# Layer 0's queries made for two blocks of 256 tokens at once

## The chip, the cores and the metric

The kernel runs on one core of one Trainium2 chip. A core has five engines that run their own instruction streams [...]: TensorE (PE in the profile, its weight loads PEld), VectorE (DVE), ScalarE (ACT), GpSimd (POOL) and SyncE (SP), which here only issues transfers. The metric is the device time of one execution in microseconds (us); lower is better.

## The reference

Two transformer layers over x of 2 sequences x 2048 tokens x 512 features, in float32. The change is in layer 0's cross-attention to a context of 128 tokens per sequence:

```
q = layer_norm(_layernorm(x), ln_g, ln_b) @ Wq      # 16 heads of 64
k, v = (layer_norm(ctx) @ Wk, layer_norm(ctx) @ Wv)
q, k = rope(q), rope(k)
aw = 30 * tanh((q . k / 8) / 30), masked (causal, padding)
x = x + (softmax(aw) @ v) @ Wo
```

Then follow a quantised feed-forward layer (its step for x is taken from the largest absolute value of all normalised tokens, so it can't start before the last token of the attention is done), and layer 1 with a second cross-attention and a feed-forward layer of eight experts.

## The kernel before

Everything is in `two_layers`. x lies in 32 SBUF tiles of 128 tokens, `xs[n]`. Layer 0's attention walks over blocks of 256 tokens (`B0`, two tiles each): 16 blocks, the two sequences in turns. A block has 4 units, one for each group `g` of 4 heads, so there are 64 units, and a loop over `u` from 0 to 65 writes down by hand the order in which PE, DVE, ACT and POOL get their instructions (`manual_schedule`); only the transfers on SP are placed by the framework. Each engine works through its list in order.

What one pass of the loop issues:

- `scores(u)` (L413): 16 small products into the first half of the PSUM tile `sc`; ACT then takes tanh (L418) and exp (L420) of them. For the first block of each sequence POOL applies the causal mask (L422).
- `queries(u + 2, par)` (L392): the queries of the unit two ahead, even and odd dimensions (`par` 0 and 1) apart. Each is 4 products of 128 features x 256 tokens (each is two instructions in the trace, since the data are float32). DVE multiplies with the rope tables (L397, L398, L401, L403), POOL combines them to `q0`, `q1` (L402, L404).
- `mixed(u - 1)` (L434): row sums and weighted values into the second half of `sc`; DVE takes the reciprocal (L440) and multiplies (L441) to `att`. `sc` is one tile, so the next scores wait for L441, and the mix waits for the tanh of the unit before it in the order.
- `projected(u - 2, t)` (L450): the unit's part of the output projection, for the block's two tiles `t`. The four units of a block are summed in one PSUM tile `pw` for each of the two tiles of tokens.
- after the last unit of a block, `finished` adds `pw` to x (L458) and takes mean and variance (L91); `largest` normalises and takes the largest absolute value (L467).

The queries need the normalised x by feature (features on partitions). For the first two blocks `first_blocks` normalises by token (`center`, L103) and PE transposes (L369), ACT adds gain and bias on the way out of PSUM (L378). For the other 14 blocks a copy of x by feature is loaded (`features_in`, 512 KB); `normed` takes the statistics, writes them through DRAM (`turned_in`, L343), and they come back spread over all partitions (`along`); POOL subtracts the mean (`centered`, L349), DVE multiplies (`scaled`, L349), ACT applies gain and bias. In between, DVE quantises the rows of the feed-forward weights (`makes`: `gate_up`, `down`; L278 to L284), 26 in all, and SP turns them by transfer into `wgT`, `wuT` and `wdT`. `steps_along` (L472, L476) spreads the down weights' steps.

After the loop, layer 1's keys (L660) fill PE while `act_step` takes the maximum over all tokens (L622 to L633), from which the feed-forward layer's first products (L743) are made ready.

Two lines that matter for the order:

```
                if u + 2 < nu:
                    queries(u + 2, 0)
                elif 1 < u < nu:
                    projected(u - 2, 0)
```

Of the kernel before, what the change touches and what calls it, by code (L numbers as in the profile page):

```python
# [54 lines left out]
NB0 = B0 // P  # L55
BF = 512
# [6 lines left out]
def two_layers(ctx: ExitStack, tc: tile.TileContext, a, out):  # L63
# [86 lines left out]
    with ExitStack() as l0:  # L150
# [16 lines left out]
        order = [b * TPB + j * NB0 + t for j in range(TPB // NB0) for b in range(B) for t in range(NB0)]  # L167
# [24 lines left out]
        for n in order[:NB0]:  # L192
            load(xs[n], x_in[n])
        xnTs = {}

        def features_in(k):

            xnTs[k] = mid.tile([P, ND, B0], F32, name="xnT", bufs=3)
            load(xnTs[k], a["x_turned"][k // B, k % B])
# [13 lines left out]
        def tables_in(j):  # L213
            tabs[j] = []
            for name in ("rope_cos", "rope_sin"):
                tab = mid.tile([P, B0], F32, name=name)
                load(tab, a[name][:, j * B0 : (j + 1) * B0])
                tabs[j].append(tab)
# [100 lines left out]
        blocks = [(j, b) for j in range(S // B0) for b in range(B)]  # L319
        tiles = [[b * TPB + j * NB0 + t for t in range(NB0)] for j, b in blocks]  # L320
        nu = len(blocks) * NG
        stats, along, ropes, qs, prs, atts, pws = {}, {}, {}, {}, {}, {}, {}
        stat_dram = dram.tile([len(blocks), NB0, 2, P], F32, name="stat_dram")
# [3 lines left out]
        def normed(k):  # L327


            stats[k] = small.tile([P, NB0, 2], F32, name="stat")  # L330
            for t, n in enumerate(tiles[k]):
                mv = variance(xs[n])
                ve = small.tile([P, 1], F32, name="ve")
                nc.vector.tensor_scalar(ve, mv[:, 1:2], 1.0 + EPS, EPS * EPS, ALU.mult, ALU.add)
                nc.vector.tensor_copy(stats[k][:, t, 0:1], mv[:, 0:1])
                nc.gpsimd.tensor_tensor(stats[k][:, t, 1:2], ve, minus_half, ALU.pow)
            if k > 1:
                features_in(k)
                turned_in(k)

        def turned_in(k):

            nc.sync.dma_start(out=stat_dram[k].rearrange("t s p -> p (t s)"), in_=stats[k].rearrange("p t s -> p (t s)"))  # L343
            along[k] = mid.tile([P, NB0, 2, P], F32, name="along", bufs=1)
            load(along[k], stat_dram[k].partition_broadcast(P))

        def by_token(k, i, op, engine):
            x = xnTs[k].rearrange("p c (t q) -> p c t q", t=NB0)
            engine.tensor_tensor(x, x, along[k][:, :, i].unsqueeze(1).to_broadcast([P, ND, NB0, P]), op)  # L349

        def centered(k):
            by_token(k, 0, ALU.subtract, nc.gpsimd)

        def scaled(k):
            by_token(k, 1, ALU.mult, nc.vector)

        def first_blocks(k):

            xn = mid.tile([P, NB0, D], F32, name="xn", tag="xnT", bufs=3)
            for t, n in enumerate(tiles[k]):  # L360
                center(xn[:, t, :], xs[n], stats[k][:, t, 0:1], stats[k][:, t, 1:2])
            xnTs[k] = mid.tile([P, ND, B0], F32, name="xnT", bufs=3)

            def rest():
                for c0 in range(0, ND, 2):
# [6 lines left out]
                    affine(k, c0, pt)  # L372
# [3 lines left out]
        def affine(k, c0, pt=None):  # L376
            for c in range(c0, c0 + 2):
                nc.scalar.activation(  # L378
                    xnTs[k][:, c, :], xnTs[k][:, c, :] if pt is None else pt[:, c - c0, :], AF.Identity, bias=lnb[:, c : c + 1], scale=lng[:, c : c + 1]
                )  # L380

        def queries(u, par):

            k, g = divmod(u, NG)
            j, b = blocks[k]
            if par == 0:
                if j not in tabs:
                    tables_in(j)
                ropes[u] = [mid.tile([P, B0], F32, name=f"rt{i}", bufs=1) for i in range(4)]
            pq, rt = psm.tile([P, B0], F32, name="pq", tag="m"), ropes[u]  # L390
            for c in range(ND):
                nc.tensor.matmul(  # L392
                    pq, wqs[c // 2][:, c % 2, par, g * P : (g + 1) * P], xnTs[k][:, c, :], start=(c == 0), stop=(c == ND - 1)
                )
            cos, sin = tabs[j]
            if par == 0:
                nc.vector.tensor_tensor(rt[0], pq, cos, ALU.mult)  # L397
                nc.vector.tensor_tensor(rt[1], pq, sin, ALU.mult)  # L398
                return
            qs[u] = [mid.tile([P, B0], F32, name=f"q{i}") for i in range(2)]  # L400
            nc.vector.tensor_tensor(rt[2], pq, sin, ALU.mult)  # L401
            nc.gpsimd.tensor_tensor(qs[u][0], rt[0], rt[2], ALU.subtract)  # L402
            nc.vector.tensor_tensor(rt[3], pq, cos, ALU.mult)  # L403
            nc.gpsimd.tensor_tensor(qs[u][1], rt[3], rt[1], ALU.add)  # L404

        def scores(u):

            k, g = divmod(u, NG)
            j, b = blocks[k]
            for par, k_ in ((0, kTe), (1, kTo)):  # L410
                for h in range(4):
                    rows = slice(32 * h, 32 * h + 32)
                    nc.tensor.matmul(  # L413
                        sc[:, h, :B0], k_[rows, g, b * T : (b + 1) * T], qs[u][par][rows, :],
# [6 lines left out]
            if j == 0:  # L421
# [5 lines left out]
        def mixed(u):  # L427

            k, g = divmod(u, NG)
            b = blocks[k][1]  # L430
            atts[u] = mid.tile([P, 2, B0], F32, name="att")
# [7 lines left out]
            rd = mid.tile([P, B0], F32, name="rd", bufs=1)  # L439
            nc.vector.reciprocal(rd, sc[:, 0, B0:])  # L440
            nc.vector.tensor_tensor(atts[u], sc[:, 1:3, B0:], rd.unsqueeze(1).to_broadcast([P, 2, B0]), ALU.mult)  # L441

        def projected(u, t):

            k, g = divmod(u, NG)
            if g == 0:
                pws[k, t] = psq.tile([P, D], F32, name="pw", tag="pw", bufs=NB0)
            pw = pws[k, t]
            for f in range(2):
                nc.tensor.matmul(  # L450
                    pw, atts[u][:, f, t * P : (t + 1) * P], wo[:, 2 * g + f, :],
                    start=(g == 0 and f == 0), stop=(g == NG - 1 and f == 1),
                )

        def finished(k, t):

            n = tiles[k][t]
            nc.vector.tensor_tensor(xs[n], xs[n], pws[k, t], ALU.add)  # L458
# [4 lines left out]
        def largest(k, t):  # L463
            n = tiles[k][t]
            xn = mid.tile([P, D], F32, name="xn1", bufs=1)
# [3 lines left out]
        def steps_along(j):  # L469

            dg = wtmp.tile([P, P], F32, name="dg", bufs=1)
# [9 lines left out]
        turns, diags = {}, {}  # L481
        nblk = len(blocks)
# [3 lines left out]
        with tc.manual_schedule(engines={E.PE, E.DVE, E.Activation, E.Pool}):  # L486
# [11 lines left out]
            queries(0, 0)  # L498
            values(1, 0)
            normed(1)  # L500
            queries(0, 1)
# [3 lines left out]
            queries(1, 0)  # L505
            queries(1, 1)
            for u in range(nu + 2):
                k, g = divmod(u, NG)
                if u < nu:
                    scores(u)  # L510
                if g == 0 and 0 < k < nblk - 1:
                    centered(k + 1)
                if u + 2 < nu:
                    queries(u + 2, 0)
                elif 1 < u < nu:
# [3 lines left out]
                if u + 2 < nu:  # L519
                    queries(u + 2, 1)  # L520
                if u > 1:
                    for t in range(0 if u + 2 < nu or u >= nu else 1, NB0):
                        projected(u - 2, t)
                if u == 0:
                    turn = first_blocks(1)
                if u == 1:
                    turn()
# [785 lines left out]
```

## Time and profile before

| what | value |
|---|---|
| three runs | 1627.55, 1620.93, 1627.21 us (median 1627.21) |
| the profiled execution | 1623.87 us, span 1622.2 us |
| granted TensorE clock, mean | 0.995 |
| PE busy | 1566.2 us (97%) in 9690 instructions |
| PEld, DVE, ACT, POOL busy | 57%, 72%, 43%, 36% |
| scores of unit 0 start | 50.27 us |
| last projection of layer 0 ends, layer 1's first keys | 674.32 us |
| first product of the feed-forward layer | 686.02 us (its first weight load) |

The page of the profile divides the span in 40 slices of 40.6 us and gives the busy share of each engine in tenths. A group of instructions is a line of the code with its shape, its busy time, the mean length of one, and the idle time ahead of it with what ended most of that. In the rows of busy time by stretch the columns are the stretch, its length, then busy time and count for PE, PEld, DVE, ACT and POOL, the granted clock, the share of the transfer engines and GB/s. The timeline gives start, length, engine, line, operation, tiles and count; in brackets the idle time before it and what ended it. Matmul ends are modelled.

### The profile page before, as it was taken

The page shows a single profiled execution, that of the slowest core. Times are in us where ns is not written, and L with a number is a line of the kernel's source. Part 1 is how long each engine was busy: PE and PEld are TensorE (multiplying, and loading weights), DVE is VectorE, ACT ScalarE, POOL GpSimd, SP SyncE. Part 2 cuts the span into 40 slices and gives each one's busy share as a digit, 9 for nine tenths or more (in the row PEclk, how much of TensorE's full clock was granted, in tenths as well). Part 3 has the DMA queues.
Part 4 walks back from the last instruction along what each step waited for, and adds up shares of the span by engine and source line. Part 5 has one row for each costly group of instructions (what it writes and reads, how often), then busy time and mean ns, then how long its engine had stood idle before and what let it go on. Part 6 is the DMA issues. An engine that isn't in the chain of part 4 may idle for free. (4 is left out here: it accounts for less than half of the span.)

```text
span 1622.2 us, 26285 instructions
## 1 busy us (share of the span) xinstructions
PE 1566.2 (97%) x9690; PEld 922.2 (57%) x9714; DVE 1160.9 (72%) x2276; ACT 694.1 (43%) x1537; POOL 583.6 (36%) x576
## 2 busy tenths in 40 slices
PE   7999999999999999999999989999999998999997
PEld 5655555655555565434444556666666665654443
DVE  3467777777777875689986678787787879766322
ACT  1222222222222222234336567676766765753332
POOL 2232222222222221110006644555656443544553
PEclk9999999999999999999999999999999999999999
DMA  9511112111111310567659650000000000113332
GB/s 323 178 37 40 46 41 55 40 46 40 47 46 36 77 37 5 160 174 189 180 168 314 221 202 20 28 21 34 27 21 27 14 21 14 40 47 108 128 121 68
DMA packets 135164, 139.64 MB, mean 86 GB/s; under 512 B 51681, under 2 KB 99257, under 8 KB 135036
## 3 DMA queue, kind: packets, MB, share of 16 engines
q1 hardware_dynamic: 125932, 118.07, 23.9%
q0 software_dynamic: 6240, 18.70, 3.6%
q8 instruction: 78, 1.28, 0.3%
q10 hardware_dynamic: 2864, 1.19, 0.3%
q14 instruction: 50, 0.41, 0.1%
HBM read 89.97 MB, written 41.79 MB: 81 GB/s over the span
## 5 line engine op out<-in xcount | busy, mean ns | idle before, releaser
L392 PE MATMUL pq<-xnT,wq 128*128 128x256 f32 x1024 | 254.4, 391 | 0.0
L418 ACT ACTIVATE pr<-sc 128x1024 f32<-128x1024 f32 x64 | 65.6, 1025 | 421.6 <-PE sc L413 421.5
L450 PE MATMUL pw<-wo,att 128*128 128x512 f32 x512 | 230.8, 593 | 0.0
L392 PEld LDWEIGHTS pq<-xnT,wq 128*128 128x128 f32 x1024 | 184.4, 189 | 67.1 <-issue 44.0
L900 POOL TENSOR_TENSOR s<-s,rs 128x1024 f32<-128x1024 f32 x64 | 132.6, 2085 | 185.1 <-DVE rs L899 184.7
L891 ACT ACTIVATE s<-s,mx 128x128 f32<-128x128 f32 x512 | 175.3, 388 | 20.8 <-DVE mx L882 20.8
L402 POOL TENSOR_TENSOR q<-rt,rt 128x256 f32<-128x256 f32 x64 | 46.8, 731 | 339.8 <-DVE rt L401 335.4
L450 PEld LDWEIGHTS pw<-wo,att 128*128 128x128 f32 x512 | 96.9, 190 | 96.4 <-issue 89.9
L440 DVE RECIPROCAL rd<-sc 128x256 f32<-128x256 f32 x64 | 112.4, 1757 | 46.6 <-PE sc L434 46.4
L1146 PE MATMUL pz<-we,x 128*128 x312 | 140.7, 594 | 0.7 <-issue 0.6
L849 PE MATMUL pq<-xT,wq 128*128 128x256 f32 x512 | 124.1, 385 | 0.1
L877 DVE SCALAR_TENSOR_TENSOR s<-sc,keep 128x1024 f32<-128x1024 f32 x64 | 78.0, 1219 | 53.5 <-PE sc L869 45.4
L932 PE MATMUL pw<-wo,oT 128*128 128x512 f32 x256 | 115.2, 592 | 0.7 <-ACT oT L923 0.7
L955 PE MATMUL pl<-wgate,xnT 128*128 128x512 f32 x256 | 115.3, 593 | 0.0
L849 PEld LDWEIGHTS pq<-xT,wq 128*128 128x128 f32 x512 | 94.8, 190 | 28.1 <-issue 13.9
L748 ACT ACTIVATE gate<-pg,gsc 128x512 f32<-128x512 f32 x88 | 60.5, 687 | 96.6 <-PE pg L743 81.4
L397 DVE TENSOR_TENSOR rt<-pq,rope_cos 128x256 f32<-128x256 f32 x64 | 27.0, 422 | 104.3 <-PE pq L392 104.3
L743 PE MATMUL pu<-xqT,wuT 128*128 128x512 bf16 x345 | 90.4, 382 | 4.2 <-DVE h L751 3.8
L91 DVE BATCH_NORM_STATS2 st<-x 128x6 f32<-128x512 f32 x130 | 89.4, 688 | 5.7 <-DMA x<-in_ctx 3.5
L1150 DVE TENSOR_TENSOR x<-x,x 128x512 f32<-128x512 f32 x39 | 27.0, 693 | 90.0 <-ACT x L1149 89.8
L743 PE MATMUL pg<-xqT,wgT 128*128 128x512 bf16 x344 | 90.1, 382 | 0.4
L1146 PEld LDWEIGHTS pz<-we,x 128*128 128x128 f32 x312 | 56.3, 190 | 58.3 <-issue 58.0
(216 smaller groups left out, 2791.9 us busy)
## 6 DMA issues: line engine op xcount, KB each, us to landing
h_dram<-h SPq DMA_DIRECT2D x88, 256.0 KB
hq<-h_dram SPq DMA_DIRECT2D x31, 704.0 KB
x_dram<-x SPq DMA_DIRECT2D x32, 258.0 KB
x<-in_x SPq DMA_DIRECT2D x32, 256.0 KB
we<-in_L_ffn_We SPq DMA_DIRECT2D x8, 1024.0 KB
xnT<-in_x_turned SPq DMA_DIRECT2D x14, 512.0 KB
along<-stat_dram SPq DMA_DIRECT2D x14, 256.0 KB
w_in<-in_L_ffn_w_gate SPq DMA_DIRECT2D x11, 256.0 KB
```

The source lines that it names most:

```text
L91: nc.vector.bn_stats(out=st, in_=x)
L392: nc.tensor.matmul(pq, wqs[c // 2][:, c % 2, par, g * P : (g + 1) * P], xnTs[k][:, c, :], start=(c == 0), stop=(c == ND - 1))
L440: nc.vector.reciprocal(rd, sc[:, 0, B0:])
L450: nc.tensor.matmul(pw, atts[u][:, f, t * P : (t + 1) * P], wo[:, 2 * g + f, :], start=(g == 0 and f == 0), stop=(g == NG - 1 and f == 1),)
L743: nc.tensor.matmul(dst, w[:, c, i * P : (i + 1) * P], xqTs[blk][:, c, :], start=(c == 0), stop=(c == ND - 1),)
L849: nc.tensor.matmul(pq, wq1[:, c, f * P : (f + 1) * P], xTs[blk][:, c, :], start=(c == 0), stop=(c == ND - 1))
L877: nc.vector.scalar_tensor_tensor(s, sc[:, 2 * half : 2 * half + 2].rearrange("p r c k -> p (r c) k"), -MASKED, keeps[n].unsqueeze(1).to_br ...
L891: nc.scalar.activation(s[:, h, :], s[:, h, :], AF.Exp, bias=mx[:, h : h + 1], **accum)
L900: nc.gpsimd.tensor_tensor(s, s, rs.unsqueeze(2).to_broadcast([P, 8, T]), ALU.mult)
L932: nc.tensor.matmul(pw, os_[n][:, c, :], wo1[:, c, :], start=(c == 0), stop=(c == ND - 1))
L955: nc.tensor.matmul(pl, xn2T[n][:, c, :], wgate[:, c, :], start=(c == 0), stop=(c == ND - 1))
L1146: nc.tensor.matmul(pz, ring[j][:, c, :], we[:, bass.ds(e, 1), c, :], start=(c == 0), stop=(c == ND - 1))
```

## The change

Two neighbouring blocks of one sequence form a superblock of 512 tokens (`BQ`): 8 superblocks, 8 units each, in the order group 0 and 1 of the first block, group 0 and 1 of the second, then groups 2 and 3 likewise. `queries(s, g, par)` works on 512 tokens, one parity of one group in each pass of the loop, four passes ahead of its first use; only for groups 0 and 1 of the first superblock the halves are made apart (32 products stay 256 columns wide). The scores, the mix and the projection keep their 256 tokens. The order of PE in a pass becomes scores, projection of the first tile, mix, queries, projection of the second tile; in the last four passes with scores there are no queries left.

Since the groups of a block are no longer neighbours, `pw` is summed over two units only and added to x twice (`added`). The first four blocks (two superblocks) are transposed by PE, the other six superblocks are loaded by feature, 1 MB each. x by feature of even superblocks lies in the place of the down weights `wdT` (`spare`), together with one half of `along`; so the down weights are quantised and turned in passes 52, 54, 56 and 59. Rope tables are 512 tokens wide with one buffer instead of two. The normalised tokens of `first_blocks` use the down weights' load buffer, and `largest` uses `sdb`.

```
+BQ = 2 * B0
+NBQ = BQ // P
...
-        order = [b * TPB + j * NB0 + t for j in range(TPB // NB0) for b in range(B) for t in range(NB0)]
+        order = [b * TPB + j * NBQ + t for j in range(TPB // NBQ) for b in range(B) for t in range(NBQ)]
...
+        spare = wdT.rearrange("p i f -> p (i f)").bitcast(F32)
...
+        def features(s):
+            if s % 2 == 0:
+                xnTs[s] = spare[:, : ND * BQ].rearrange("p (c t) -> p c t", c=ND)
+            else:
+                xnTs[s] = mid.tile([P, ND, BQ], F32, name="xnT", bufs=1)
...
-                tab = mid.tile([P, B0], F32, name=name)
-                load(tab, a[name][:, j * B0 : (j + 1) * B0])
+                tab = mid.tile([P, BQ], F32, name=name, bufs=1)
+                load(tab, a[name][:, j * BQ : (j + 1) * BQ])
...
+        units = [(s, half, 2 * q + g) for s in range(nsb) for q in range(NG // 2) for half in range(2) for g in range(2)]
...
+        def queries(s, g, par, half=None):
+
+            j = s // B
+            cols = slice(0, BQ) if half is None else slice(half * B0, (half + 1) * B0)
+            if j not in tabs:
+                tables_in(j)
+            if (s, g) not in qs:
+                qs[s, g] = [mid.tile([P, BQ], F32, name=f"q{i}", bufs=3) for i in range(2)]
+            pq = psm.tile([P, BQ], F32, name="pq", tag="m")[:, cols]
             for c in range(ND):
                 nc.tensor.matmul(
-                    pq, wqs[c // 2][:, c % 2, par, g * P : (g + 1) * P], xnTs[k][:, c, :], start=(c == 0), stop=(c == ND - 1)
+                    pq, wqs[c // 2][:, c % 2, par, g * P : (g + 1) * P], xnTs[s][:, c, cols], start=(c == 0), stop=(c == ND - 1)
                 )
...
-            rd = mid.tile([P, B0], F32, name="rd", bufs=1)
+            rd = att[:, 1, :]
...
+        def added(u, t):
+
+            s, half, _ = units[u]
+            n = tiles[2 * s + half][t]
+            nc.vector.tensor_tensor(xs[n], xs[n], pws[u, t], ALU.add)
...
+            queries(0, 1, 0, 0)
+            firsts[0] = first_blocks(1)
+            queries(0, 1, 1, 0)
             for u in range(nu + 2):
-                k, g = divmod(u, NG)
+                s, i = divmod(u, nus)
                 if u < nu:
                     scores(u)
...
+                if u in firsts:
+                    firsts[u]()
+                if u < 2:
+
+                    for par in range(2):
+                        queries(0, u, par, 1)
+                if u > 1:
                     projected(u - 2, 0)
                 if 0 < u <= nu:
                     mixed(u - 1)
...
+                if u > 1 and i % 2 == 1:
+                    added(u - 2, 0)
+                if u + nus // 2 < nu:
+                    v, w = divmod(u + nus // 2, nus)
+                    queries(v, *divmod(w, 2))
                 if u > 1:
...
+                    projected(u - 2, 1)
+                    if i % 2 == 1:
+                        added(u - 2, 1)
...
+                if 1 < s + 1 < nsb:
+                    if i in (1, 3):
+                        affine(s + 1, i - 1)
+                    if i in (0, 2):
+                        scaled(s + 1, i)
+                    if i == 0:
+                        centered(s + 1, 2)
+                if u == 1:
+                    normed(2)
+                    firsts[2] = first_blocks(2)
+                if u == 2:
+                    normed(3)
+                    firsts[3] = first_blocks(3)
+
+                done = (2 * s - 1 if i == 1 else 2 * s) if i in (1, nus - 1) else None
+                if done is not None and done >= 0:
                     for t in range(NB0):
-                        finished(k - 1, t)
-                    largest(k - 1, 0)
...
+                    if i == 4:
+                        features_in(s + 2)
+                        normed(2 * (s + 2))
+                    if i == 5:
+                        normed(2 * (s + 2) + 1)
+                        turned_in(s + 2)
+                if i == nus - 1 and 1 < s + 2 < nsb:
+                    centered(s + 2, 0)
+                late = makes and makes[0][0] is down_in
+                if makes and (u in (52, 54, 56, 59) if late else u > 2 and i in (0, 3, 4, 6)):
```

## The prediction

> **What bounds the kernel now.** I read the page's slices first: TensorE is full from the second slice to the seventeenth, which is layer 0's attention (scores of the first unit at 50.27 us, last projection up to 674.32 us), at full granted clock.
> ```profile
> PE   7999999999999999999999989999999998999997
> ...
> PEclk9999999999999999999999999999999999999999
> ```
> Then busy time by stretch, one unit (four heads of one block) per row: PE busy equals the stretch, early and late alike, while DVE needs 4.5 to 5.9 us of 9.79. The last row is a unit without queries: there PE has gaps (6.63 of 7.23).
> ```profile
> 83.14:92.93 9.79, 9.79 (x65) 5.79 (x65) 5.73 (x12) 2.36 (x4) 4.37 (x4) 1.00 0.00 0
> ...
> 308.31:318.10 9.79, 9.79 (x65) 5.80 (x65) 5.73 (x11) 2.17 (x2) 2.19 (x3) 1.00 0.01 3
> ...
> 651.40:658.63 7.23, 6.63 (x51) 3.14 (x51) 5.64 (x12) 2.71 (x4) 1.33 (x2) 1.00 0.40 150
> ```
> So layer 0 costs what its PE instructions cost, and anything that makes PE wait is added in full. The timeline divides a unit (308.31 to 318.10): scores 1.08, first query half 1.92, mix 1.43, second query half 1.83, projections 3.53 us.
>
> **The change part by part.**
>
> *Queries, 512 columns instead of 256.* The build's order has 240 such products of 512 columns and 32 of 256, for 512 of 256. The page's groups suggest a gain:
> ```profile
> L392 PE MATMUL pq<-xnT,wq 128*128 128x256 f32 x1024 | 254.4, 391 | 0.0
> ...
> L450 PE MATMUL pw<-wo,att 128*128 128x512 f32 x512 | 230.8, 593 | 0.0
> ```
> By busy time a narrow instruction is 254.4/1024 = 0.248 us, a wide one 230.8/512 = 0.451: a wide one in place of two saves 45 ns, 480 times, 21.8 us. [...] What PE pays is the distance between starts, which the weight loads show (each starts as its forerunner's matmul does):
> ```profile
> 309.71 0.19 PEld L392 LDWEIGHTS pq<-xnT,wq 128*128 128x128 f32 x1
> 309.92 0.19 PEld L392 LDWEIGHTS pq<-xnT,wq 128*128 128x128 f32 x1
> ...
> 315.00 0.19 PEld L450 LDWEIGHTS pw<-wo,att 128*128 128x128 f32 x1 [0.24 <-issue]
> 315.43 0.19 PEld L450 LDWEIGHTS pw<-wo,att 128*128 128x128 f32 x1 [0.24 <-issue]
> ```
> 0.215 us at 256 columns (five more follow at that pace), 0.43 at 512: exactly double, and the 0.19 us load is under it in both. [...] I take 0. The changes of tile shape, which cost some 0.1 to 0.2 us each, stay four to a unit (scores, projection, mix, query, projection): 1.08 + 1.91 + 1.43 + 3.55 + 1.81 = 9.78. The rhythm stays 9.79.
>
> *Other steady work.* The rope's 512-wide DVE operation I price by L441 (512 columns from PSUM, 0.691): 1.38 us a unit for 1.66. The sums into x double (32 more at 0.682, 22 us). DVE's longest unit, the first of eight, has 2.5 (reciprocal and product) + 1.4 + 1.25 (scaling) + 1.25 (largest) + 3 to 4 (weight quantising) = about 10 us, the eight together some 67 of 78.3. Scores wait for the product of the mix; that ends 2.5 us before them, so DVE may lag 2.5; I find a lag of up to 1.6, made up in the next unit: 0, with a bound of 2.5 us in 6 superblocks, 15. The PSUM bank of the first projection is freed a unit earlier than needed. x by feature: stat_dram took 8.1 to 10.1 us for 512 single words and now has 1024, at most 20; along is then there about 26 us after the write is issued, GpSimd is at its centering 23 us after it, DVE needs the result 29 after: 0. The rope tables have one buffer now, and SP issues them behind the 1 MB of x; 1.5 MB at the 352 to 383 GB/s of 670 to 672 us is 4.3 us, DVE needs them 8 us into the unit: 0. Queued behind these on SP are only the next weight rows, wanted a unit later.
>
> *The start* (u = 0 to 3; before: 50.27 to 83.14, 32.9 us). Two more blocks are turned by PE (16 transposes, 2.2 us), and, more important, their normalising now stands in DVE's order behind the rope of a query that PE finishes only at the end of a unit, while the transposes stand right behind the next scores. Prices:
> ```profile
> 52.54 1.15 ACT L420 ACTIVATE pr<-pr,pad 128x1024 f32<-128x1024 f32 x1
> ...
> 55.78 1.79 DVE L103 TENSOR_SCALAR xn<-x,stat 128x512 f32<-128x512 f32 x2
> ...
> 61.26 0.60 PE L369 MATMUL pt<-ident,xn 128*128 128x128 f32 x4
> ...
> 61.90 1.02 ACT L378 ACTIVATE xnT<-pt,lnb,lng 128x256 f32<-128x256 f32 x2 [3.48 <-PE pt L369]
> ...
> 62.98 0.66 PE L369 MATMUL pt<-ident,xn 128*128 128x128 f32 x4 [1.11 <-ACT xnT L378]
> ```
> - u = 0: the first superblock's second half is queried right after its transposes; they end at about 52.45, ACT is at tanh and exp until 53.7 and empties the first bank at 54.7: PE waits 2.4 us. The unit: 1.08 + 1.1 + 2.4 + 3.5 (two half-width parities) + 3.5 (one full) = 11.6.
> - u = 1: 1.08 + 3.65 + 1.43 + 3.55 = 9.7.
> - u = 2: from its start DVE does rope 1.6, two variances at 1.08 (to 3.7), GpSimd two combinations of q (I take 1.2 us for 512 words, between L402's 0.73 at 256 and L900's 2.09 at 1024) and two powers at 0.55 (to 4.5), DVE the second centering to 5.5. PE has been through with the scores at 1.08: a wait of 4.5 us. Then 1.1 + 1.83 + 1.43 + 3.55 + 1.81: 15.3 in all.
> - u = 3: query's end at 13.5, rope to 15.2, variances to 17.3, centering to 19.0; scores end at 16.4: a wait of 2.7, the unit 13.6.
>
> Sum 50.2, so 17.3 us more, 7.2 of which is that queries run two units further ahead. If the centering were covered, 7.2 less.
>
> *The end.* Before, only the last two units lack queries, now four: they save 7.2 us of PE work but are then bound by the loop scores, mix, reciprocal, product, scores: 1.08 + 1.92 + 1.43 + 2.82 = 7.25 (the row above: 7.23). From scores(59) to the end of mix(62): before 621.59 to 663.08, 41.5. After: 9.79, then 8.45 (the last down weights' 4.6 us of quantising delays the reciprocal), 7.25, 7.25, 4.44: 37.2, a gain of 4.3. Then:
> ```profile
> 665.92 0.64 PE L434 MATMUL sc<-pr,ones 128*32 128x256 f32 x8 [0.63 <-DVE att L441]
> ...
> 667.35 7.13 PE L450 MATMUL pw<-wo,att 128*128 128x512 f32 x16
> ...
> 672.80 0.69 DVE L458 TENSOR_TENSOR x<-x,pw 128x512 f32<-128x512 f32 x1 [2.85 <-PE pw L450]
> ```
> Before, the last reciprocal starts at once and the maximum over all tokens (DVE, L622) at 679.03, 15.95 us after mix(62). After, DVE has two sums, two variances and a maximum of block 14 ahead of that reciprocal (product done at 10.0 instead of 6.9), the last projection ends at 13.65 instead of 11.24, and both sums precede both variances; the maximum starts at 20.1. A loss of 4.1. The layer-1 context load now waits for the last mix (6.9) and has 6.7 us to land, in which 512 KB take some 4: 0.
>
> *Sum:* +17.3 - 4.3 + 4.1 = +17.1 us; what follows layer 0 has the same instructions. The profiled execution, 1623.87 us (span 1622.2), becomes 1641.0. The median of the three runs, 1627.21, lies 3.3 higher; with it 1644.3. I forecast 1642.5.
>
> *Clock.* [...] The granted clock reads 1.00 in every early row, but after the idle time of 9.5 to 10.9 us the keys' loads are 0.43 us apart at 256 columns, twice the later distance, for some 5 us:
> ```profile
> 11.07 0.76 PEld L252 LDWEIGHTS pk<-x,x 128*128 128x128 f32 x2
> 11.50 0.76 PEld L252 LDWEIGHTS pk<-x,x 128*128 128x128 f32 x2
> ```
> [...] by the rows of gaps under 2 us nothing. [...] I take 0 [...].
>
> **Rivals.**
> - *Wide products are really cheaper* (not slower): place, the 480 query instructions; price 45 ns each by busy time, -21.8, so 1620.7 with the median between, about as before; it decides from 17.1/480 = 36 ns. For it speaks the groups' busy time, against it the distance of starts. [...]
> - *The start is mostly covered:* waits of 2.4 + 4.5 + 2.7 shrink to some 2 us: +9, 1634.
> - *DVE or the transfers miss the beat once or twice a superblock*, since x by feature, tables and quantising meet in the same units: 2 to 5 us in each of 6, +12 to +30, 1655 to 1672. For it speaks DVE's fuller order, against it the 2.5 us of slack.
> - The change does what it says: widths, order and places stand in the build.
>
> **How the numbers follow.** Forecast 0.62 (1636 to 1650 with the clock), start covered 0.14 (1627 to 1636), missed beat 0.15, wide products cheaper 0.09. Range 1630 to 1656. 0.5% is 8 us, about what a measurement can tell from no change. Slower: forecast, missed beats and half of the covered start, 0.83; same: the rest of that and half of the cheap products, 0.12; faster 0.05.
>
> **What would show it.** Distance of query loads 0.43; units of 9.79 from u = 4 to 59; PE waiting for DVE xn ahead of the transposes at two places (4.5 and 2.7 us) and for ACT once; units 60 to 63 near 7.3; the maximum some 20 us after mix(62). Wrong if units in the middle are shorter than 9.7 us, or if long PE waits recur every eight units.

## The result and the profile after

The changed kernel takes 1638.62 us (median of five runs, 1636.81 to 1640.20), the kernel before 1623.52 us in the same five rounds: ratio 1.0089, 95% interval 1.0066 to 1.0112. It is slower by 15 us. The forecast was 1642.5 us, range 1630 to 1656, and the likeliest case (slower through the start of layer 0) is the one that came. The profiled execution took 1638.62 us with a span of 1636.9 us, 14.7 us longer than that of before. One of e5's fourteen executions below took 2697 us at a mean granted clock of 0.56; its ratio is formed without it.

Divided at the same events in both traces (PE's start of scores, the end of a mix as the start of what follows it, DVE's maximum over all tokens, the first matmul of the feed-forward layer):

| stage | before | after | difference | forecast |
|---|---|---|---|---|
| to the first scores | 50.27 | 49.97 | -0.30 | 0 |
| u = 0 to 3 | 32.87 | 51.81 | +18.94 | +17.3 |
| scores(4) to scores(59) | 538.45 | 537.34 | -1.11 | 0 |
| scores(59) to the end of mix(62) | 41.49 | 35.89 | -5.60 | -4.3 |
| mix(62) to the maximum | 15.95 | 18.62 | +2.67 | +4.1 |
| maximum to the first feed-forward product | 7.42 | 9.10 | +1.68 | 0 |
| the rest | 935.75 | 934.17 | -1.58 | 0 |
| sum | 1622.2 | 1636.9 | +14.70 | +17.1 |

The slices of the page, 40.9 us each, hardly show it: two more digits of PE's row are 8, the second (the start) and the seventeenth (the end), and the granted clock is at 9 throughout.

The groups of the query products show how busy time misleads. Columns as before: busy time, mean ns, idle time ahead.

```profile
L410 PE MATMUL pq<-wdT,wq 128*128 128x512 f32 (+1 forms) x288 | 118.2, 555 | 2.2 <-ACT wdT L396 2.2
L410 PE MATMUL pq<-xnT,wq 128*128 128x512 f32 x256 | 118.4, 605 | 0.0
...
L471 PE MATMUL pw<-wo,att 128*128 128x512 f32 x512 | 249.6, 611 | 2.1 <-DVE x L480 1.1
```

Together the two query groups are 236.6 us busy where the 1024 narrow ones were 254.4: 17.8 us "saved". But the projections, the same 512 instructions as before, now take 249.6 us where they took 230.8 (e3 below says why). The 55 steady units (u = 4 to 58), which hold 440 of the 480 wide instructions, became 1.11 us shorter. Busy time by stretch for these units (start and length, then PE, PEld, DVE, ACT, POOL, clock, transfers), after:

```profile
101.78:639.12 537.34, 537.34 (x3081) 235.25 (x3080) 389.24 (x679) 136.62 (x136) 133.01 (x126) 1.00 0.17 43
```

and before:

```profile
83.14:621.59 538.45, 538.45 (x3521) 318.69 (x3521) 418.13 (x778) 147.41 (x168) 151.04 (x182) 1.00 0.18 44
```

PE is without a gap in both, with 440 instructions fewer after; weight loads fell by 83 us of busy time and DVE by 29, and neither was on the path.

The start is where the time went. PE's timeline after, u = 0, 2 and 3:

```profile
54.34 7.15 PE L410 MATMUL pq<-wdT,wq 128*128 128x256 f32 x24 [2.21 <-ACT wdT L396]
...
75.80 0.33 PE L386 MATMUL pt<-ident,xn 128*128 128x128 f32 x1 [3.44 <-DVE xn L105]
76.42 1.31 PE L386 MATMUL pt<-ident,xn 128*128 128x128 f32 x7 [0.29 <-DVE xn L105]
77.52 3.29 PE L471 MATMUL pw<-wo,att 128*128 128x512 f32 x4
...
89.93 0.30 PE L386 MATMUL pt<-ident,xn 128*128 128x128 f32 x1 [1.27 <-ACT pr L438]
90.83 1.75 PE L386 MATMUL pt<-ident,xn 128*128 128x128 f32 x7 [0.60 <-DVE xn L105]
92.37 2.69 PE L471 MATMUL pw<-wo,att 128*128 128x512 f32 x4
```

The three waits stand where they were forecast: for ACT at u = 0 and for the normalised block at u = 2 and 3 (one is put down to `pr`, which ends at 89.8 as DVE's first centering does; it is the centering that the transposes read). Each of the last two is cut in two by a first transpose, 3.44 + 0.29 and 1.27 + 0.60 us. But the projections behind them are also long: 4 instructions of 512 columns take 1.88 us elsewhere, here 3.29 and 2.69. Busy time by stretch, cut to 3.41 us, shows why: in the clock's column (the eighth figure, 1.00 elsewhere in these units) it is 0.50 for exactly one such stretch behind u = 2's wait and one behind u = 3's:

```profile
53.03:56.44 3.41, 2.10 (x10) 1.87 (x11) 0.07 (x1) 2.17 (x5) 0.64 (x1) 1.00 0.66 252
73.52:76.93 3.41, 0.84 (x6) 0.66 (x7) 2.30 (x8) 1.15 (x1) 2.26 (x3) 1.00 0.00 0
76.93:80.34 3.41, 3.41 (x9) 1.60 (x7) 0.00 (x0) 1.93 (x4) 0.00 (x0) 0.50 0.00 0
87.17:90.58 3.41, 1.79 (x18) 0.86 (x17) 2.83 (x11) 1.77 (x2) 1.39 (x2) 1.00 0.00 0
90.58:93.99 3.41, 3.16 (x9) 2.23 (x10) 0.19 (x1) 2.33 (x5) 0.00 (x0) 0.50 0.17 21
```

The first row holds most of the wait of u = 0, which was not followed by half rate.

The end, PE's timeline after:

```profile
678.35 1.98 PE L471 MATMUL pw<-wo,att 128*128 128x512 f32 x4 [1.13 <-DVE x L480]
...
684.65 3.70 PE L471 MATMUL pw<-wo,att 128*128 128x512 f32 x8 [0.97 <-DVE att L462]
...
694.36 5.31 PE L701 MATMUL pk<-ctxT,wq 128*128 128x256 f32 x16
```

and DVE's:

```profile
682.12 1.75 DVE L461 RECIPROCAL att<-sc 128x256 f32<-128x256 f32 x1
...
693.63 0.19 DVE L663 TENSOR_REDUCE m<-amax 128x1 f32<-128x32 f32 x1
```

The last projection of unit 62 waits for the sum that empties its bank, the last mix stands behind it, and the last reciprocal follows block 14's statistics on DVE. The 16 key products after the maximum take 5.31 us; before, the same 16 took 3.62, behind an idle time of 1.68 us in place of 2.42. The clock is 0.50 again, from 694.74 on for 3.41 us.

### The profile page after: what moved, and what is told of

Same layout as the page of the kernel before. It is cut to its first block, busy times and chain, and to the rows that moved or that the text cites. A ratio compares the mean times of both kernels' runs of the same rounds, so it can differ in the third digit from the quotient of the medians.

```text
span 1636.9 us, 24946 instructions
## 1 busy us (share of the span) xinstructions
PE 1569.6 (96%) x9226; PEld 834.6 (51%) x9250; DVE 1142.0 (70%) x2190; ACT 686.7 (42%) x1513; POOL 563.2 (34%) x514
## 5 line engine op out<-in xcount | busy, mean ns | idle before, releaser
L471 PE MATMUL pw<-wo,att 128*128 128x512 f32 x512 | 249.6, 611 | 2.1 <-DVE x L480 1.1
L461 DVE RECIPROCAL att<-sc 128x256 f32<-128x256 f32 x64 | 112.5, 1758 | 113.9 <-PE sc L454 113.9
L421 POOL TENSOR_TENSOR q<-q,rt 128x512 f32<-128x512 f32 (+1 forms) x34 | 41.0, 1204 | 365.9 <-DVE rt L420 365.9
L471 PEld LDWEIGHTS pw<-wo,att 128*128 128x128 f32 x512 | 92.6, 192 | 115.5 <-issue 102.4
L410 PE MATMUL pq<-wdT,wq 128*128 128x512 f32 (+1 forms) x288 | 118.2, 555 | 2.2 <-ACT wdT L396 2.2
L410 PE MATMUL pq<-xnT,wq 128*128 128x512 f32 x256 | 118.4, 605 | 0.0
L410 PEld LDWEIGHTS pq<-wdT,wq 128*128 128x128 f32 x288 | 52.4, 190 | 56.9 <-issue 53.1
```

The costliest lines, as they stand in the source:

```text
L410: nc.tensor.matmul(pq, wqs[c // 2][:, c % 2, par, g * P : (g + 1) * P], xnTs[s][:, c, cols], start=(c == 0), stop=(c == ND - 1))
L471: nc.tensor.matmul(pw, atts[u][:, f, t * P : (t + 1) * P], wo[:, 2 * g + f, :], start=(g % 2 == 0 and f == 0), stop=(g % 2 == 1 and f == 1),)
```

## The experiments

Times are medians; the kernel before ran beside each (1623.05 to 1624.49 us). The theory: nothing is to be had from the wide products, and all that was lost lies in the start and the end, by the order of DVE's work, by queries that run further ahead, and by PE's half rate after it stood idle. The main rival: wide products do save busy time's 45 ns each, and larger losses hide it. In e5 and e7 to e10 the first transposes stand ahead of the scores of u = 0, and the last column counts from them on.

| run | us | ratio to before, 95% interval | u = 0 to 3 |
|---|---|---|---|
| changed kernel | 1638.62 | 1.0066 to 1.0112 | 51.81 |
| e1, blocks normalised earlier | 1630.08 | 1.0026 to 1.0059 | 43.60 |
| e2, idle products in the waits | 1635.32 | 1.0060 to 1.0097 | 48.61 |
| e3, products of 256 columns | 1640.50 | 1.0085 to 1.0121 | 54.42 |
| e4, order of the end, three key groups | 1641.65 | 1.0101 to 1.0139 | 51.85 |
| e5, start in another order | 1629.64 | 1.0030 to 1.0047 | 42.86 |
| e6, end, idle products | 1635.97 | 1.0063 to 1.0101 | 51.96 |
| e7, e5 and e6, lead of three | 1653.31 | 1.0173 to 1.0201 | 38.14 |
| e8, e7 and superblock 1 by feature | 1651.87 | 1.0160 to 1.0194 | 35.72 |
| e9, start by feature, end, lead of four | 1624.10 | 0.9991 to 1.0009 | 39.16 |
| e10, as e9, lead of three, query first | 1622.88 | 0.9980 to 0.9996 | 35.73 |

**e1: the order of the normalising.**

```
                 if u in firsts:
                     firsts[u]()
+                if u == 1:
+                    normed(2)
+                    normed(3)
+                    firsts[2] = first_blocks(2)
+                if u == 2:
+                    firsts[3] = first_blocks(3)
...
-                if u == 1:
-                    normed(2)
-                    firsts[2] = first_blocks(2)
-                if u == 2:
-                    normed(3)
-                    firsts[3] = first_blocks(3)
```

> The changed kernel, with the statistics and the normalising of blocks 2 and 3 written ahead in DVE's order: block 2 right behind the scores of u = 1, block 3 right behind its predecessor's transposes at u = 2, both before the rope of the late query. If the order of DVE's work made the start dear: no wait ahead of the transposes, u = 2 and u = 3 take 1.08 + 1.1 + 1.83 + 1.43 + 3.55 + 1.81 = 10.8 us each in place of 16.30 and 14.26, 9.0 us less, so about 1629.6 us. If DVE has simply too much to do in these units, the wait moves to the rope or the reciprocal of u = 1 to 3 and no more than 3 us are gained: 1636 to 1639 us.

Measured: 1630.08, 8.5 us less. PE's timeline:

```profile
68.92 3.70 PE L410 MATMUL pq<-wdT,wq 128*128 128x512 f32 x8 [1.07 <-DVE q L417]
...
73.63 1.10 PE L386 MATMUL pt<-ident,xn 128*128 128x128 f32 x8
...
84.23 1.09 PE L386 MATMUL pt<-ident,xn 128*128 128x128 f32 x8
```

The transposes of u = 2 and 3 have no wait and full rate (10.61 and 10.60 us a unit, 10.8 expected). About an eighth of the gain came back as a new wait of 1.07 us in u = 1: the rope, which frees the PSUM bank, now stands behind 5.2 us of normalising. So the order of DVE's work was the cause of the two long waits, and of the half rate behind them.

**e2: PE kept busy in the same waits.** In `first_blocks`, ahead of the first transposes of blocks 2 and 3:

```
+                    if c0 == 0:
+                        for _ in range({2: 4, 3: 2}.get(k, 0)):
+                            nc.tensor.matmul(
+                                pt.rearrange("p c t -> p (c t)"), wqs[0][:, 0, 0, :P], xnTs[0][:, 0, :], start=True, stop=True
+                            )
```

> The changed kernel, with idle products put ahead of the transposes of u = 2 (8 instructions of 512 columns, 3.4 us) and u = 3 (4, 1.7 us), into a PSUM tile that the transposes then overwrite: the waits for the normalised block stay, but PE is busy in them. If the half-rate loads after the waits (0.86 us apart in place of 0.43) come from PE having been idle, they are gone: u = 2 takes about 14.9 us in place of 16.30, u = 3 about 12.9 in place of 14.26, 2.7 us less, about 1636 us. If the half rate has another cause (a port or transfer that the projection shares), the units stay at 16.3 and 14.3 and the time at 1638.6.

Measured: 1635.32; u = 2 takes 14.62 and u = 3 12.73 us, 1.68 and 1.53 less, with 12 instructions more. The timeline of PE in u = 2:

```profile
77.28 0.98 PE L391 MATMUL pt<-ident,xn 128*128 128x128 f32 x7 [0.29 <-DVE xn L105]
78.10 1.88 PE L476 MATMUL pw<-wo,att 128*128 128x512 f32 x4
```

The transposes come as late after the scores as they did; only the half rate behind them is gone (1.88 us in place of 3.29), and the granted clock is 1.00 throughout the start. Half rate came from the idle time here, and cost 3.2 us in the start. The profiled executions of e4 and e6, whose start is the changed kernel's, have the half rate at both places, as that one has.

**e3: the width alone.**

```
-            for c in range(ND):
-                nc.tensor.matmul(
-                    pq, wqs[c // 2][:, c % 2, par, g * P : (g + 1) * P], xnTs[s][:, c, cols], start=(c == 0), stop=(c == ND - 1)
-                )
+            for h0 in range(cols.start, cols.stop, B0):
+                for c in range(ND):
+                    nc.tensor.matmul(
+                        pq[:, h0 - cols.start : h0 - cols.start + B0], wqs[c // 2][:, c % 2, par, g * P : (g + 1) * P],
+                        xnTs[s][:, c, h0 : h0 + B0], start=(c == 0), stop=(c == ND - 1)
+                    )
```

> The changed kernel, with every query product of 512 columns made as two of 256 into the two halves of the same PSUM tile; order, rope and all else unchanged. If PE pays the distance of starts (0.43 us at 512 columns, 0.215 at 256), the units of u = 4 to 59 stay at 9.77 within 0.1 us and the time within 2 us of 1638.6. If a wide product saves 45 ns against two narrow ones, as busy time says, 480 of them cost 21.8 us more: units of 10.2 us, 1660 us.

Measured: 1640.50, 1.9 us more, not 21.8. The scores of two neighbouring units are 9.79 us apart, the figure of before, and those of u = 4 and 59 (103.99 and 642.44) 538.45, to the digit what the kernel before needs:

```profile
632.65 0.71 PE L434 MATMUL sc<-q,kTe 32*128 32x256 f32 x8
...
642.44 0.71 PE L434 MATMUL sc<-q,kTe 32*128 32x256 f32 x8
```

So the width is worth 1.11 us over 440 instructions, 2.5 ns each. The rival that wide products are cheaper is out. Where the busy time went is shown by PE's busy time in the steady units, for the query products alone and the projections alone:

| u = 4 to 58 | query products | projections | all of PE |
|---|---|---|---|
| before, 256 columns | 219.34 | 197.80 | 538.45 |
| e3, 256 columns | 204.64 | 212.47 | 538.45 |
| changed, 512 columns | 203.54 | 212.48 | 537.34 |

For e3's query products the row is (length, PE alone with the count, then clock and transfers):

```profile
103.99:642.44 538.45, 204.64 (x880) 1.00 0.18 43
```

With the old width in the new order, 14.7 of the 15.8 us are "saved" just the same, and the projections gain 14.7. A matmul's modelled end lies behind the start of the next one (0.59 us long, 0.43 apart), so each unbroken run of a group carries busy time beyond its starts, 0.27 us here by the projections' rise (14.67/55). Before, a unit had two runs of queries and one of projections; now it has one and two. So most of the page's 17.8 us is the order of PE's work, not the width.

In this profiled execution the start is longer (54.42 us), though nothing in it but the width differs: the wait for ACT in u = 0, 2.21 us as in the changed kernel, was followed by half rate here (more in the last section).

**e4: the order of the end.** The last mix ahead of unit 62's projection, `finished` and `largest` of block 14 in the pass after, and `for f in range(3): keys(f)` ahead of the maximum in place of 2:

```
-                if u > 1:
+                if 1 < u != nu:
                     projected(u - 2, 0)
                 if 0 < u <= nu:
                     mixed(u - 1)
+                if u == nu:
+                    projected(u - 2, 0)
...
+                done = None if u == nu - 1 else 2 * s - 2 if u == nu else done
```

> The changed kernel with two edits at the end, read apart by stage. (1) the last mix stands ahead of unit 62's projection, and block 14's statistics and first maximum stand behind the last reciprocal and product. If DVE's order there cost the time: end of mix(62) to the maximum over all tokens 17.2 us in place of 18.62 (DVE without its 1.9 us of idle time); if DVE is full there anyhow, 18.6. (2) three of layer 1's four key groups stand ahead of the maximum in PE's order in place of two. If the 16 key products at half rate (5.31 us in place of 3.62) come from the idle stretch of 2.4 us before them: maximum to first feed-forward product at most 7.4 us in place of 9.10; if not, 9.1. Together 3.1 us less or more, about 1635 us, or no change.

Measured: 1641.65, 3.0 us more. The first edit did what was expected: mix(62) to the maximum 17.12 us. The second could not be read, since it set off something else. Behind the loop DVE's order is the framework's, and with the keys moved it put the scaling of the expert biases ahead of the maximum's second half (`gm`), where it waits for its load:

```profile
699.17 0.22 DVE L773 TENSOR_SCALAR vrow<-vrow 36x128 f32<-36x128 f32 x1 [6.29 <-DMA vrow<-in_L_ffn_bg]
```

Maximum to the first product became 14.0 us.

**e6: the end again, with idle products.** As e4, but with two key groups; idle products in `act_step`; and the row of the expert biases is computed so that nothing waits early for its load:

```
+        for _ in range(9 if column_maxima is amax1 else 0):
+            nc.tensor.matmul(pm, ident, ident, start=True, stop=True)
         nc.tensor.transpose(pm, mb, ident)
...
-        nc.vector.tensor_scalar(vrow, vrow, 1.0 / (ND * RAISE), None, ALU.mult)
-        nc.vector.scalar_tensor_tensor(vrow, wrow[:, 0, :], -1.0 / ND, vrow, ALU.mult, ALU.add)
+        nc.vector.tensor_scalar(wrow[:, 0, :], wrow[:, 0, :], -1.0 / ND, None, ALU.mult)
+        nc.vector.scalar_tensor_tensor(vrow, vrow, 1.0 / (ND * RAISE), wrow[:, 0, :], ALU.mult, ALU.add)
```

> The changed kernel with the end's order of the earlier run (last mix ahead of unit 62's projection, block 14's statistics and first maximum behind the last product), the key groups back at two and two, and 18 idle products of 128 columns (about 1.9 us) between the first two key groups and the transpose of the maximum; the scaling of the expert biases' row, which stood ahead of the maximum's second half on DVE and waited for its load, is folded into a later instruction. DVE's order: mix(62) to maximum 17.1 us (18.62 in the changed kernel). Half rate from an idle PE: the second 16 key products take 3.6 us in place of 5.3, maximum to first feed-forward product 7.4 in place of 9.10. In all 3.2 us less, about 1635.4. If the half rate comes from something else, only 1.5 less.

Measured: 1635.97, 2.7 us less. mix(62) to the maximum 17.11, maximum to the first product 7.35 us, and the second 16 key products:

```profile
693.38 3.62 PE L706 MATMUL pk<-ctxT,wq 128*128 128x256 f32 x16
```

Full rate again: 1.5 us of the end was DVE's order, and 1.7 in the profiled execution the half rate. The latter is not lost in every execution: in the profiled ones of e1, e3 and e5, without idle products, the idle time ahead of the maximum was not followed by half rate either (7.42 us to the first product; it was 9.11 in e2 and 9.10 in the changed kernel). With idle products it was 7.35 in all five, e6 to e10. So that the idle products are what keeps the rate up is shown in the start, by e2, and here only made likely.

**e5: the start in a third order.** `firsts[0]()` ahead of `scores(0)`; `normed(2)`, `normed(3)` and the normalising of block 2 in u = 0 behind them.

> The changed kernel with a third order of the start: the transposes of block 1 stand ahead of the first scores, and the statistics of blocks 2 and 3 and the normalising of block 2 in u = 0, where DVE has 5.5 us without work. If all that is dear in the start is order: u = 0 takes 9.5 us in place of 11.46 (PE does not wait for ACT, which empties the transposes before the first tanh), u = 1 9.8, u = 2 and u = 3 10.6 each, in all 40.5 in place of 51.8: 11.3 us less, about 1627.3. What stays against the kernel before (32.9) would be the queries that run two units further ahead (7.1) and one more pair of transposes than its start has. If ACT's tanh, now behind the emptying, delays the mix of u = 1, or the data of blocks 2 and 3 are not there yet, 3 us or more of it stay.

Measured: 1629.64, 9.0 us less, of the 11.3 expected; u = 0 took 11.86 us. It doesn't wait for ACT any more, but for the rope behind the normalising:

```profile
57.48 3.70 PE L410 MATMUL pq<-wdT,wq 128*128 128x512 f32 x8 [1.77 <-DVE q L417]
```

The 5.5 us in which DVE had no work in the changed kernel lay in PE's wait for ACT and the queries behind it; without that wait, the normalising (50.2 to 56.8 us in e5) takes longer than the queries that hide it (52.0 to 55.7). u = 1 to 3 took 9.79, 10.61 and 10.60 as expected.

**e7 and e8: a lead of three passes.** e7 is e5 and e6 with `queries` called for `u + 3` in place of `u + 4`; e8 also loads superblock 1 by feature.

> Both orders together (start and end), and the queries made three passes ahead in place of four, so that one query product fewer stands at the start (3.53 us) and one unit more has one at the end (9.77 in place of some 7.25): 11.3 + 3.2 + 1.1 = 15.6 us less than the changed kernel, about 1623, level with the kernel before. If the queries of group 1, now finished one pass before their scores, come late (rope and its sums on GpSimd), 1 to 3 us in each of eight superblocks are lost: 1630 or more.

> As the run before, but the second superblock (blocks 2 and 3) is loaded by feature as the later ones are, so that PE has 16 transposes fewer: u = 2 and u = 3 take 9.8 each in place of 10.6, 1.7 us less, about 1621. If the statistics, which go through memory, or the 1 MB of x come too late for the queries of u = 5, the wait appears there and the time is above that of the run before.

Both missed by far: 1653.31 and 1651.87, where about 1623 and 1621 were expected. The waits of PE in layer 0 of e7 (in total, times, longest):

```profile
PE sc L432 <- POOL q L423: 13.7, 15, 1.5
PE sc L432 <- POOL q L421: 7.0, 15, 0.5
```

Twice in each superblock the query of the second group ends one 1.8 us projection ahead of the scores that need it, and behind it stand 0.69 us of rope and two sums of 1.27 us on GpSimd. So the fourth pass of lead is not spare in this order. In e8, u = 2 and 3 did fall to 9.77, but ACT took gain and bias of superblock 1 ahead of the tanh of u = 4, whose mix waited:

```profile
92.31 1.08 PE L454 MATMUL sc<-pr,ones 128*32 128x256 f32 x8 [2.79 <-ACT pr L438]
```

**e9 and e10: what is left of the change when the start and the end are put right.** e9: the changed kernel with e6's end, e5's order in u = 0, and superblock 1 by feature with its centering and scaling a pass earlier than in e8. e10: also the lead of three, with `queries` straight behind `scores`:

```
+                asked = 1 < u < nu - 3
+                if asked:
+                    v, w = divmod(u + 3, nus)
+                    queries(v, *divmod(w, 2))
+                if 1 < u != nu and not asked:
                     projected(u - 2, 0)
                 if 0 < u <= nu:
                     mixed(u - 1)
+                if 1 < u and (asked or u == nu):
+                    projected(u - 2, 0)
+                if u == 1:
+                    queries(0, 2, 0)
...
-                if u + nus // 2 < nu:
-                    v, w = divmod(u + nus // 2, nus)
-                    queries(v, *divmod(w, 2))
```

> The changed kernel with its lead of four passes, the end of the run with the idle products, the start with the transposes of block 1 ahead of the first scores, and blocks 2 and 3 loaded by feature (subtracted in u = 1, scaled in u = 2, gain and bias in u = 3, so that ACT does not hold up the mix of u = 4, where it took 2.79 us in the run before). u = 0 to 3 from the first transpose on: 9.9 + 9.8 + 9.8 + 9.8 = 39.3 us in place of 51.8, which is 12.5 less, and 2.7 less from the end as measured: about 1623.4, level with the kernel before (1623.3). If the second superblock's x by feature still comes late, PE waits in u = 4 or 5 and the time is 1625 or more. What can be had against the kernel before is then only the 1.1 us by which the wide products shorten the steady units.

> As the run beside it, but with a lead of three passes and the query product straight behind the scores, ahead of the mix, so that rope and GpSimd's sums have 5 us before the next scores. If the 20.7 us of waits for GpSimd in the earlier run with a lead of three came from the 1.8 us that lay between the query product and the next scores, they are gone and one query product at the start (3.54 us) is exchanged for 2.5 us at the end: about 1622.4. If the mix's reciprocal and product, now 3.6 us ahead of the next scores instead of 5.4, come late instead, 1 us or more is lost in each pass: 1680.

Measured: e9 1624.10 (ratio 1.0000), e10 1622.88 (ratio 0.9988). e9's start takes 39.16 us: the 32.87 of before, plus two query products of 3.53, plus a wait of 0.34 for the rope at the second transposes, less the wait of 1.11 for ACT that the start of before has. Up to the first feed-forward product e9 is level (686.14 us, before 686.45): these 6.3 us more stand against 1.0 ahead of the start, 1.1 in the steady units and 4.5 at the end. e10's takes 35.73, one product less, and its stretch from scores(59) to mix(62) 38.51 in place of 35.89; PE waits for GpSimd nowhere in it. Each came within 0.7 us of its expectation. e10 is faster than both kernels, by 1.6 us against before (0.6 to 3.2 by the interval). The traces account for little of that: up to the first feed-forward product it needs 685.97 us and the kernel before 686.45. What follows takes 931.5 us (e8) to 939.9 us (e10) in the twelve profiled executions, though the work is the same. Half rate is part of that: behind the first feed-forward product e10's trace has four steps of 3.41 us at 0.50 and e8's none, up to 6.8 us by an estimate from half the rate. The rest stays unassigned.

## Why the prediction was right, step by step

- **What bounds the kernel, and the price of a query product: right, and e3 shows it.** The step "what PE pays is the distance between starts" decided the sign. In the trace of before the starts are 0.216 us apart at 256 columns and 0.429 at 512, and the query load at 309.71 us starts together with the matmul ahead of it. The saving is 2.5 ns for each wide instruction, 1.11 us over the 440 of u = 4 to 58; I had taken 0. The "0.1 to 0.2 us" at a change of tile shape is what the groups of that unit take beyond their starts: 0.20 and 0.11 us for the query halves (1.92 and 1.83 for 8 starts of 0.215), 0.09 for the projections (3.53 for 8 of 0.43). That a float32 product is two instructions shows in the counts of before: 1024 for the 512 query products, where the feed-forward layer's 352 bf16 products for `pg` left 344 records. The 45 ns were hardly a price of width: in the kernel before a run of 8 narrow products is busy for 1.99 us with 8 starts of 0.216 us, a run of 8 wide ones for 3.60 us with 8 of 0.429. It is the 0.26 and 0.17 us beyond the starts that, spread over 8 instructions each, make 45 ns between two narrow ones and a wide one.
- **Other steady work at 0: right.** From u = 4 to the last scores with queries PE has no wait at all. From the issue of a write of 1024 single words to that of the load behind it 8.5 to 11.4 us passed (forecast: at most 20; before, with 512, it was 8.2 to 10.8), and PE waited for nothing in these units.
- **The start: right in place and cause, +18.9 for +17.3.** Sized term by term: the two queries further ahead 7.1 (forecast 7.2); 16 more transposes 1.7 (2.2), by the 0.84 us that e1's u = 2 and 3 take above the steady 9.77; the waits 2.21, 3.73 and 1.87 us (less 1.11 that the kernel before waited in its start) where 2.4, 4.5 and 2.7 were forecast (by the forecast's own times, 54.7 less 52.45, the first is 2.25; DVE was through with the second centering 5.1 us into u = 2, not 5.5, and 3.3 into u = 3, not 3.7); and the half rate, 3.2 us by e2, which was taken as 0. These make 18.7. The two errors, -1.8 and +3.2, partly cancelled.
- **The clock: the term that was mis-sized.** It was taken as 0, and cost 3.2 us in the start and 1.7 ahead of the feed-forward layer, 4.9 us in the profiled execution. That the longer waits might cost more, as the "1636 to 1650 with the clock" allows for, was my estimate; no row of before showed how much. What the rows of gaps under 2 us show is full clock after the idle times of 1.11 us at 61.9 to 63.0 us and of 1.68 us ahead of the maximum. But an idle time's length is not all that counts (last section): half rate followed the waits of 1.87 us in u = 3, which had been left out of the account, and of 2.42 us ahead of the maximum, and not the 2.21 us of u = 0. One reading behind the 0 was wrong: "1.00 in every early row" says nothing of the keys' loads at 11 us, since the record of the granted clock in that trace begins only at 16.0 us.
- **The end: -5.6 for -4.3.** The step that failed is unit 60's 8.45 us: the last down weights were to delay the reciprocal, but the unit took 7.36. The next two took 7.17 (7.25).
- **mix(62) to the maximum: +2.7 for +4.1**, the same mechanism with the last product done 9.6 us after mix(62) in place of 10.0 and the last projection 13.2 in place of 13.65. e4 and e6 won 1.5 of it back by order; for the other 1.2 DVE is the bound: in e6 it stands idle for only 0.5 us between its last sums of block 14 and the maximum.
- **Rivals.** Wide products cheaper: refuted by e3. Start mostly covered: no, though e1 shows that it needed only another order. A missed beat in the steady units: none here; e7 shows what one costs (20.7 us) as soon as the lead is one pass shorter.

The forecast of the profiled execution was 1641.0, measured 1638.62: of the 2.4, 1.6 lies behind layer 0, where nothing was changed and executions vary (931.5 to 939.9 us in the twelve profiled ones). That it came so close is in part luck: the half rate, taken as 0, added 4.9 us, and shorter waits, a shorter unit 60, the earlier maximum and the 1.1 us of the steady units took back more than that.

## What to carry to other kernels

Price a wider matmul by the distance of starts in a dense stretch, not by the busy time of its group, which also changes with how often other work breaks its run: here it fell by 17.8 us, the time by 1.1, and most of the 17.8 turned up again at the projections. If the rhythm can't get shorter, a change that makes work further ahead costs what it puts at the start and gives back less at the end, so what stands at both ends decides (here e9 and e10 got the 15 us back there, and hardly anything beyond them). When an idle stretch on TensorE can't be removed, putting products into it that nobody needs can still pay: in e2 the four projection instructions behind the first wait then took 1.88 us in place of 3.29.

## What the runs showed of the hardware that I had not expected

TensorE fell to half rate after idle times of 3.73, 1.87 and 2.42 us in the changed kernel, and the 2.21 us in u = 0 led to it in e3's profiled execution and not in the changed kernel's. Each spell at 0.50, but for the last one, which runs past the last product to the end of the execution, lasted 3.41 us or a multiple of it (6.83 in e3, e9 and e10, 10.24 in e4), and their starts lie on a grid of 3.413 us: in the changed kernel 90.58 and 694.74 us are 4 and 181 steps behind 76.93 (13.65 and 617.81 us), and so it is in all twelve traces, where the grid lies at another place in each. So in these traces the clock changed only at times on such a grid, and whether it fell went with how busy PE was in the step before. PE's busy time in the steps of the changed kernel: 0.84, 1.79 and 0.99 us were followed by 0.50; 2.10 (u = 0) and, in the kernel before, 1.99 us ahead of its maximum were not. In e3 the grid lay otherwise, and the 2.21 us of idle time in u = 0 fell into one step:

```profile
51.95:55.36 3.41, 1.41 (x7) 1.26 (x8) 0.00 (x0) 2.86 (x5) 0.64 (x1) 1.00 0.77 291
55.36:58.77 3.41, 3.41 (x10) 2.69 (x9) 0.76 (x2) 0.00 (x0) 0.00 (x0) 0.50 0.00 0
```

These few cases suggest a sharp limit near 1.9 us, but there is none in busy time. Over the whole of the twelve traces (5603 steps at full clock), all 16 steps with up to 1.43 us of busy time were followed by 0.50 and none of the 5547 with 1.80 us or more; of the 40 between, 15 were and 25 were not. This step of e5, in its u = 0, was not:

```profile
55.01:58.43 3.42, 1.65 (x6) 0.76 (x5) 2.42 (x6) 0.00 (x0) 2.75 (x6) 1.00 0.04 14
```

So busy time, with its modelled ends, is not quite what decides; what does, no run here shows. A step at half rate costs up to 1.7 us by an estimate, half of its length; without it e2's u = 2 and u = 3 were 1.68 and 1.53 us shorter. By a further estimate from these figures, an idle time above some 1.6 us (3.41 less 1.80) is a chance of 1.7 us more, and the times of one kernel can spread by that much.
